# Gated cross-attention layer: the row table made by ScalarE before the branch, counting of places for slots two to four by six comparisons, and a changed order at the start

## The chip, the cores and the metric

The kernel runs on one NeuronCore of a Trainium2 chip. The metric is the time of one execution on the device, in microseconds (us). Before the change it is 656.4 us, the median of three runs (655.87 to 658.57). Engines are named as the profile names them: PE is TensorE (its weight loads are listed as PEld), DVE is VectorE, ACT is ScalarE, POOL is GpSimd, and SP only issues DMAs.

## The reference

There are 16 batches. Each has 224 rows of x (512 features) and a context of 750 rows (384 features), of which a mask keeps some. The layer is cross-attention with a gate, then a feed-forward network with weights rounded to -1, 0, 1 and rows rounded to 8 bits, with a second gate:

```python
sim  = einsum('bihd,bjhd->bhij', q, k) * 64**-0.5        # q from layernorm(x), k and v from the context
sim  = where(mask[:, None, None, :], sim, -finfo.max)
out  = einsum('bhij,bjhd->bihd', softmax(sim), v) @ W_o + b_o
x    = x + tanh(g_xattn) * out
# bitlinear: act_quant(rmsnorm(x)) against weight_quant(w), then + b
x    = x + tanh(g_ffn) * bitlinear(gelu(bitlinear(layernorm(x), w1, b1)), w2, b2)
```

`weight_quant` scales a whole weight matrix by the mean of its absolute values, so all of w1 must have been loaded and summed before any of it can be rounded; the same holds for w2.

## The kernel before, in words

**Sorting the batches.** `order_batches` loads the mask, counts the kept context rows of each batch and sorts the batches by that count. Position s in the sorted list is called slot s. `CAPS` gives each slot a number of context rows that it may use at most. A number `n_odd` tells whether all batches fit; every engine loads it (line 436) and branches on it (line 437). With these inputs the compact path is taken.

Only kept context rows are fetched. For slot s a table `upto` holds running counts of kept rows, in six parts of 125 rows (`NJ` = 6). The step `ind` compares the places 0 to 191 with that table, the step `pi` lets PE sum the comparisons over partitions, and the step `keys` makes row numbers of the sums. POOL then gathers these rows by an indirect DMA (`fetch_keys`, line 1055). Rows of x are gathered in sorted order in the same way (`fetch_x`, line 975), from a table `token`, which is made from `slots` by `spread` and one DVE operation (lines 265 to 270 and 343).

**Slot 0** is handled before the branch by `first_slot` (lines 1030 to 1055): six comparisons into six tiles; then for each half (128 and 64 places) six matmuls into one column of the PSUM tile `pi_0`, a DVE operation that makes the half's keys, and the gather. For the **other slots** `ind` is one comparison (line 1080) and five that also add what is there already (line 1082), into one tile with a single buffer; `pi` is then one matmul for each half (line 1091), and `keys` is line 1105.

**After the branch** the order of all work is written out by hand, as a string of step names (`ORDER`). Each step issues its instructions, its DMAs too, on the engines it uses, and every engine works through its own instructions in that order. A tile can be reused only when its readers are done. Steps that matter here:

- `hold.0` lets ACT read the first gathered context row, so that the loads after it on SP (`load.wv`, then `w.0.0` to `w.0.7`, the eight 512 KB pieces of w1) do not start before that gather has landed.
- `tokens` makes the token table on DVE. `stats.0.0`, `stats.0.1`, `rstd`, `norm.0.0` and `norm.0.1` normalise the first two tiles of x (lines 1258 to 1272); the power of -1/2 in it is POOL's (line 1267).
- `x.2.0` and other `x` steps are gathers of x, `ctx.1.0` and other `ctx` steps are gathers of context. All of them are issued by POOL.
- `warm` is eight matmuls whose result nobody uses (line 2137). `xnp` and `ctxp` are PE transposes of x and context (lines 1323 and 1160); `qp`, `kp` and `vp`/`vr` are the projections (lines 1345, 1180, 1207, 1224); `sim` are the scores (line 1378).
- `ws.0.*` sum the pieces of w1, some on ACT (line 2009) and some on DVE (line 2006). `wt.0` adds the sums, `wtp.0` is PE's matmul over partitions (line 2024) and `sw.0` makes the scale. After it come the rounding on DVE (`wi`, `wq`, lines 2047 and 2053), DMA transposes (`wd`, line 2061) and copies into `w1T` (`wT`). The same is done for w2 afterwards, in the same eight buffers; its `wtp.1` stands about 34 us later.

From there on the attention of a slot, the output projection and the feed-forward network of pairs of row tiles run interleaved to the end.

Of the kernel before, what the change touches and what calls it, by code (L numbers as in the profile page):

```python
# [10 lines left out]
BF16 = mybir.dt.bfloat16  # L11
AF = mybir.ActivationFunctionType
ALU = mybir.AluOpType
# [13 lines left out]
CAPS = (188, 188, 184, 180, 176, 168, 156, 148, 128, 124, 116, 104, 92, 80, 64, 64)  # L27

ORDER = """
hold.0 load.wv tokens stats.0.0 stats.0.1 rstd.0.0 rstd.0.1 x.2.0 norm.0.0 norm.0.1 ind.1 warm xnp.0 xnp.1 xnT.0.0:s  # L30
xnT.1.0:s xnT.1.1:s gap mask.0 ctxp.0.2 ctxp.0.0 qp.0.0 pi.1 ctxT.0.0:s ctxT.0.2:s keys.1 w.0.0 w.0.1 w.0.2 w.0.3
w.0.5 w.0.7 w.0.4 w.0.6 x.2.1 ctx.1.0 kp.0.0 ind.2 pi.2 x.1.0 x.1.1 ind.3 ws.0.1:s keys.2 stats.2.1 ctx.2.0 tanh
ws.0.0:v x.3.0 kp.0.2 kT.0.0:s stats.2.0 qT.0.0:s kT.0.0.c:s stats.1.1 rstd.2 ws.0.3:s sim.0.1 ws.0.2:v sim.0.0
ctx.1.1 kT.0.2:s ws.0.5:s vp.0 max.0.0.0 max.0.0.1 max.0.0.3 kT.0.2.c:s stats.1.0 exp.0.0.0 exp.0.0.1 max.0.1.0 rstd.1
exp.0.0.3 vr.0 max.0.0.2 v.0:s max.0.1.3 exp.0.0.2 norm.1.0 ws.0.4:v qp.0.2 v_rest.0:s norm.1.1 ws.0.7:s rec.0.0
# [172 lines left out]
def order_batches(ctx, tc, sh, mask, x, loads, fetch, first_slot):  # L208

    nc = tc.nc  # L210
    P = 128
    B, J = mask.shape
    S = x.shape[1]
    NJ = 6
    TJ = J // NJ
# [45 lines left out]
    for p, q, t in bounds:  # L261
        numbers(at[p:q, :, t : t + 1], [[7 * P - 4 * S, 4]], p + t * P - (t + 1) // 2 * S, 1)

    def spread(dst, src, on):

        by4 = src.rearrange("p (g s) -> p g s", s=4)
        on.tensor_copy(dst.rearrange("p g (s two) -> p g s two", two=2), by4.unsqueeze(3).to_broadcast([P, 4, 4, 2]))

        for p, q, t in bounds:
            on.tensor_copy(dst[p:q, :, t : t + 1], by4[p:q, :, (t + 1) // 2 : (t + 1) // 2 + 1])  # L270

    m = sel.tile([B, J], F16, name="m")
    kept = sel.tile([B, 1], F32, name="kept_of")
# [57 lines left out]
    spare = ps.tile([P, P], F32, name="spare")  # L331
    for k in range(3):
        nc.tensor.matmul(spare, lhsT=sh.ones, rhs=sh.ones, start=True, stop=True)
    first_slot(sel, ps)
    numbers(sh.place_f[:, :192], [[1, 192]], 0, 0)
    numbers(sh.place_f[:, 192:], [[1, P]], 0, 0)
    nc.gpsimd.memset(sh.mhalf, -0.5)
    where = const.tile([P, 4, 8], F32, name="where")
    sh.token = const.tile([P, 4, 8], mybir.dt.int32, name="token")

    def tokens():
        spread(where, sh.slots[:, 1, :], nc.vector)
        nc.vector.scalar_tensor_tensor(
            sh.token.rearrange("p g t -> p (g t)"),
            where.rearrange("p g t -> p (g t)"),
            float(S),
            at.rearrange("p g t -> p (g t)"),
            ALU.mult,
            ALU.add,
        )  # L350

    sh.tokens = tokens


class Shared:
# [3 lines left out]
@with_exitstack  # L359
def flamingo_gated_kernel(  # L360
    ctx: ExitStack,
    tc: tile.TileContext,
    x: bass.AP,
    context: bass.AP,
    mask: bass.AP,
    g_xattn: bass.AP,
    g_ffn: bass.AP,
    w_q: bass.AP,
    w_k: bass.AP,
    w_v: bass.AP,  # L370
    w_o: bass.AP,
    b_o: bass.AP,
    w1: bass.AP,
    b1: bass.AP,
    w2: bass.AP,
    b2: bass.AP,
    out: bass.AP,
):
    nc = tc.nc
    P = 128  # L380
    D = x.shape[2]
    C = context.shape[2]
    FF = w1.shape[0]
    ND, NC, NF = D // P, C // P, FF // P

    sh = Shared()
    sh.FF, sh.D = FF, D
    sh.const = const = ctx.enter_context(tc.tile_pool(name="const", bufs=1))
    sh.w1_dram, sh.w2_dram = w1, w2


    sh.ident = const.tile([P, P], F32, name="ident")
    sh.ident16 = const.tile([P, P], BF16, name="ident16")
    sh.ones = const.tile([P, P], F32, name="ones")
    sh.mhalf = const.tile([P, 2], F32, name="mhalf")
    sh.wk = const.tile([P, NC, D], F32, name="wk_sb")
    sh.wv = const.tile([P, NC, D], F32, name="wv_sb")
    sh.wq = const.tile([P, ND, D], F32, name="wq_sb")
    sh.wo = const.tile([P, ND, D], F32, name="wo_sb")
    sh.w1T = const.tile([P, ND, FF], F8, name="w1T")  # L400
    sh.w2T = const.tile([P, NF, D], F8, name="w2T")
    sh.bo = const.tile([P, D], F32, name="bo_bc")
    sh.b1 = const.tile([P, FF], F32, name="b1_bc")
    sh.b2 = const.tile([P, D], F32, name="b2_bc")
    sh.tgates = const.tile([P, 2], F32, name="tgates")
    sh.gates = gates = const.tile([P, 2], F32, name="gates")

    def loads():
        nc.sync.dma_start(sh.wq, w_q.rearrange("(c p) i -> p c i", p=P))
        nc.sync.dma_start(sh.wk, w_k.rearrange("(c p) i -> p c i", p=P))  # L410
        nc.sync.dma_start(gates[:, 0:1], g_xattn.partition_broadcast(P))
        nc.sync.dma_start(gates[:, 1:2], g_ffn.partition_broadcast(P))

    def late_loads(crossed):
        nc.sync.dma_start(sh.bo, b_o.partition_broadcast(P))
        nc.sync.dma_start(sh.b2, b2.partition_broadcast(P))
        by = w_o.rearrange("(c p) i -> p c i", p=P)
        if crossed:

            h = P // 2  # L420
            nc.sync.dma_start(sh.wo[:, 0:2, :], by[:, 0:2, :])
            nc.sync.dma_start(sh.wo[:h, 2:4, :], by[h:, 2:4, :])
            nc.sync.dma_start(sh.wo[h:, 2:4, :], by[:h, 2:4, :])
        else:
            nc.sync.dma_start(sh.wo, by)
        nc.sync.dma_start(sh.b1, b1.partition_broadcast(P))

    def load_wv():
        nc.sync.dma_start(sh.wv, w_v.rearrange("(c p) i -> p c i", p=P))

    stages = []
    compact = compact_path(ctx, tc, sh, x, context, out, dict(w_o=w_o, b_o=b_o, b1=b1, b2=b2, wv=load_wv), stages)
    with tc.manual_schedule(), ExitStack() as stage:
        fetch, first_slot = next(compact)
        order_batches(stage, tc, sh, mask, x, loads, fetch, first_slot)
    n_odd = nc.values_load(sh.n_odd[0:1, 0:1], min_val=0, max_val=2 * x.shape[0])
    with tc.If(n_odd == 0) as few:
        with ExitStack() as stage:
            stages.append(stage)
            next(compact, None)  # L440
    with few.Else():
        with ExitStack() as stage:
            late_loads(False)
            load_wv()
            sh.tokens()
            dense_path(stage, tc, sh, x, context, mask, out)


# [475 lines left out]
def compact_path(ctx, tc, sh, x, context, out, late_rows, stages):  # L924
# [67 lines left out]
    def rows_of(s, t):  # L992
        return min(width(s) - t * P, P)
# [38 lines left out]
    def first_slot(sel, ps):  # L1032
        ind = sel.tile([TJ, NJ, 192], BF16, name="ind_0")
        for n in range(NJ):
            nc.vector.tensor_scalar(ind[:, n, :], sh.place[:TJ], sh.upto[:, n, 0:1], None, ALU.is_ge)
        pi = ps.tile([P, 2], F32, name="pi_0")
        live[0]["ctx"] = kept = early[:, 2 * D : 2 * D + 2 * C].rearrange("p (t c) -> p t c", t=2)
        keys = sh.const.tile([P, 2], I32, name="keys_0")
        for t in range(2):
            rows = rows_of(0, t)  # L1040
            for n in range(NJ):
                nc.tensor.matmul(
                    pi[:rows, t : t + 1],
                    lhsT=ind[:, n, t * P : t * P + rows],
                    rhs=sh.one[:, 0:1],
                    start=(n == 0),
                    stop=(n == NJ - 1),
                )
            nc.vector.tensor_scalar(
                keys[:rows, t : t + 1], pi[:rows, t : t + 1], float(J - 1), sh.first[:rows, 0:1], ALU.min, ALU.add  # L1050
            )
            fetch_keys(kept[:rows, t, :], keys[:rows, t : t + 1])

    def fetch_keys(dst, at):
# [6 lines left out]
            oob_is_err=False,  # L1061
        )

    def select(s):
        if s == B - 1:
            return
# [7 lines left out]
        if s > 0:  # L1074
            @step("ind", s)
            def run():
                st["ind"] = ind = pa.tile([TJ, 192], BF16, tag="ind", name=f"ind_{s}", bufs=1)
                for b, at in parts:
                    place = sh.place[:TJ, : at.stop - at.start]
                    nc.vector.tensor_scalar(ind[:, at], place, sh.upto[:, 0, b : b + 1], None, ALU.is_ge)  # L1080
                    for n in range(1, NJ):
                        nc.vector.scalar_tensor_tensor(
                            ind[:, at], place, sh.upto[:, n, b : b + 1], ind[:, at], ALU.is_ge, ALU.add
                        )

            @step("pi", s)
            def run():
                st["pi"] = gen([P, 2], F32, f"pi_{s}")
                for t in range(nt):
                    rows = rows_of(s, t)  # L1090
                    nc.tensor.matmul(
                        st["pi"][:rows, t : t + 1],
                        lhsT=st["ind"][:, t * P : t * P + rows],
                        rhs=sh.one[:, 0:1],
                        start=True,
                        stop=True,
                    )

            @step("keys", s)
            def run():  # L1100
# [1032 lines left out]
    @step("warm")  # L2133
    def run():
        spare = gen([P, P], F32, "warm")
        for k in range(8):
            nc.tensor.matmul(spare, lhsT=sh.ones, rhs=sh.ones, start=True, stop=True)

    @step("tokens")
    def run():  # L2140
        sh.tokens()

    @step("load", "wv")
    def run():
# [71 lines left out]
```

## Time and profile before

| what | value |
|---|---|
| median of three runs | 656.4 us (655.87 to 658.57) |
| the profiled execution, its own time | 658.56 us |
| its span in the profile | 656.8 us |
| PE busy | 633.6 us, 96% |
| DVE busy | 494.2 us, 75% |
| ACT busy | 434.7 us, 66% |
| POOL busy | 380.8 us, 58% |
| PE busy between 100 and 650 us | 547.0 of 550 us |
| PE busy between 0 and 40 us | 30.1 of 40 us |

The span is what the profile covers; the execution's own time is 1.8 us longer. An idle stretch is put down to what ended it. PE's idle time lies almost wholly in the first 72 us: between 100 and 650 us it idles for 3 us. In a line of the timeline the first number is the start of a group of like instructions in us, the second its length; in square brackets stands how long the engine sat idle before it and what it waited for.

### The profile page before, as it was taken

How to read it: one execution, taken by the hardware profiler on the slowest of the kernel's cores; microseconds unless marked ns; L12 is line 12 of the kernel's file. 1: busy time of each engine (PE TensorE's matmuls, PEld its weight loads, DVE VectorE, ACT ScalarE, POOL GpSimd, SP SyncE). 2: the span in 40 equal slices, each digit the busy share in tenths (PEclk: the TensorE clock that was granted, in tenths of full speed). 3: DMA queues.
4: the chain of work that ended last, by engine and by line, in shares of the span. 5: the costliest groups of instructions: out<-in, count | busy, mean ns of one | idle time of the engine just before them, and what ended most of it. 6: DMA issues, size and time to landing. Idle time of an engine off the chain costs nothing.

```text
span 656.8 us, 11053 instructions
## 1 busy us (share of the span) xinstructions
PE 633.6 (96%) x3706; PEld 411.8 (63%) x3706; DVE 494.2 (75%) x1325; ACT 434.7 (66%) x985; POOL 380.8 (58%) x531
## 2 busy tenths in 40 slices
PE   6989899999999999999999999999999999999995
PEld 5767757767566585675756668656666755654442
DVE  6798788776874787777878577886595865858994
ACT  2489786767676673596757467875496554859694
POOL 6444558664866447663757763753776364564741
PEclk9999999999999999999999999999999999999999
DMA  6959682116233053312235521513243041433222
GB/s 204 371 81 304 196 199 69 45 49 110 66 87 86 32 80 91 84 34 61 65 77 80 96 75 34 92 46 58 64 117 73 17 97 50 95 65 81 48 33 86
DMA packets 97346, 60.73 MB, mean 92 GB/s; under 512 B 85461, under 2 KB 85609, under 8 KB 97152
## 3 DMA queue, kind: packets, MB, share of 16 engines
q1 hardware_dynamic: 89232, 35.41, 25.8%
q0 software_dynamic: 8048, 24.53, 12.4%
q8 instruction: 31, 0.51, 0.3%
q14 instruction: 35, 0.29, 0.1%
HBM read 31.87 MB, written 7.34 MB: 60 GB/s over the span
## 4 chain that ended last, share of the span: by engine, by line
PE 84%; DVE 6%; DMA 5%; ACT 2%; issue 1%; POOL 1%; DVEq 0%; POOLq 0%
PE hp L1671 14%; PE fp L1908 14%; PE qp L1345 14%; PE op L1547 13%; PE kp L1180 5%; PE vp L1207 5%; PE sim L1378 5%; PE ptp L1448 3%; PE av L1488 3%; DMA raw<-w 2%; PE xnp L1323 2%; DMA raw<-in_L_ffn_w_dram 2%; PE vr L1224 1%; DMA x<-in_x_dram,token 1%; PE ctxp L1160 1%
## 5 line engine op out<-in xcount | busy, mean ns | idle before, releaser
L1426 POOL TENSOR_TENSOR p<-p,rec 112x752 f32<-112x752 f32 (+13 forms) x64 | 73.2, 1149 | 134.4 <-DVE rec L1421 101.6
L1409 ACT ACTIVATE p<-p,nm 112x188 f32<-112x188 f32 (+13 forms) x256 | 102.0, 401 | 26.8 <-DVE nm L1395 25.8
L1345 PE MATMUL qp<-xnT,wq_sb 128*128 128x224 f32 x512 | 103.2, 355 | 0.0
L1671 PE MATMUL hp<-w1T,xqT 128*128 128x512 fp8e4 x448 | 102.1, 379 | 1.1 <-DVE h L1682 0.7
L1908 PE MATMUL fp<-w2T,hqT 128*128 128x512 fp8e4 x448 | 100.9, 379 | 0.7 <-ACT hqT L1713 0.7
L1547 PE MATMUL op<-wo_sb,xoT 128*128 128x512 f32 x224 | 101.0, 596 | 0.0
L1345 PEld LDWEIGHTS qp<-xnT,wq_sb 128*128 128x128 f32 x512 | 95.4, 190 | 4.9 <-issue 2.9
L1682 DVE SCALAR_TENSOR_TENSOR h<-hp,c,b_bc 128x1024 f32<-128x1024 f32 x52 | 66.6, 1282 | 31.3 <-PE hp L1671 26.5
L1671 PEld LDWEIGHTS <-xqT 128*128 128x128 bf16 x448 | 43.5, 98 | 51.3 <-issue 3.4
L1908 PEld LDWEIGHTS <-hqT 128*128 128x128 bf16 x448 | 43.1, 98 | 49.9 <-issue 1.1
L1547 PEld LDWEIGHTS op<-wo_sb,xoT 128*128 128x128 f32 x224 | 41.0, 190 | 44.7 <-issue 43.5
L1395 DVE CUSTOM_DVE_ANT_0 p<-sim,mask 112x64 f32<-112x64 f32 (+12 forms) x224 | 54.9, 281 | 18.7 <-PE sim L1378 12.0
L1731 DVE TENSOR_REDUCE a<-h 128x1 f32<-128x2048 f32 x26 | 59.2, 2277 | 1.1 <-ACT h L1726 1.1
L1726 ACT ACTIVATE h<-h 128x2048 f32<-128x2048 f32 x26 | 49.7, 1913 | 11.6 <-DVE h L1682 11.4
L1180 PE MATMUL kp<-ctxT,wk_sb 128*128 128x188 f32 (+12 forms) x360 | 52.4, 295 | 0.9 <-ACT pT L1025 0.9
L1180 PEld LDWEIGHTS kp<-ctxT,wk_sb 128*128 128x128 f32 x360 | 49.2, 191 | 5.9 <-issue 3.3
L1025 ACT COPY pT<-ptp 128x448 f32<-128x448 f32 (+6 forms) x54 | 28.1, 528 | 32.1 <-PE ptp L1448 30.1
L1409 ACT ACTIVATION_READ_ACCUMULATOR p<-p,nm 112x1 f32 x256 | 48.7, 190 | 0.0
L1757 ACT ACTIVATE h<-h 128x2048 f32<-128x2048 f32 x25 | 47.8, 1911 | 1.0 <-DVE hq L1737 1.0
L1378 PE MATMUL sim<-kT,qT 64*112 64x188 f32 (+13 forms) x512 | 42.5, 296 | 0.9 <-ACT xoT L1025 0.6
L1646 POOL TENSOR_TENSOR y<-y,b_bc 128x512 f32<-128x512 f32 x28 | 36.1, 1295 | 12.1 <-DVE xoT L1023 9.4
L1207 PE MATMUL vp<-wv_sb,ctxT 128*128 128x512 f32 (+5 forms) x90 | 41.6, 598 | 0.0
(211 smaller groups left out, 1161.4 us busy)
## 6 DMA issues: line engine op xcount, KB each, us to landing
raw<-in_L_ffn_w_dram SPq DMA_DIRECT2D x16, 512.0 KB, 5.5
wq_sb<-in_L_xattn_W_q_dram SPq DMA_DIRECT2D x1, 1024.0 KB
b_bc<-in_L_ffn_b_dram SPq DMA_DIRECT2D x1, 1024.0 KB
wk_sb<-in_L_xattn_W_k_dram SPq DMA_DIRECT2D x1, 768.0 KB
wv_sb<-in_L_xattn_W_v_dram SPq DMA_DIRECT2D x1, 768.0 KB
wo_sb<-in_L_xattn_W_o_dram SPq DMA_DIRECT2D x1, 512.0 KB, 11.6
wo_sb<-in_L_xattn_W_o_dram SPq DMA_DIRECT2D x2, 256.0 KB
out_dram<-y SPq DMA_DIRECT2D x2, 256.0 KB
```

The source lines that it names most:

```text
L1180: nc.tensor.matmul(pk[:, p - p0, :], lhsT=sh.wk[:, c, p * P : (p + 1) * P], rhs=st["ctxT"][:, c, :n], start=(c == 0), stop=(c == NC - 1),)
L1207: nc.tensor.matmul(pv[:w], lhsT=st["ctxT"][:, c, :w], rhs=sh.wv[:, c, :], start=(c == 0), stop=(c == NC - 1))
L1345: nc.tensor.matmul(pq[:, i, :], lhsT=sh.wq[:, d, (p + i) * P : (p + i + 1) * P], rhs=st["xnT"][:, d, :], start=(d == 0), stop=(d == ND - 1),)
L1378: nc.tensor.matmul(sim[:, j, i, :cap], lhsT=st["qT"][j * DH : (j + 1) * DH, p, q * TQ : (q + 1) * TQ], rhs=keys["kT"][j * DH : (j + 1) * D ...
L1395: nc.vector.tensor_tensor_reduce(out=probs[:, h, :cap], in0=box["sim"][:, j, i, :cap], in1=keys["mask"][:, first + j * begin : first + j * ...
L1409: nc.scalar.activation(box["p"][:, h, :cap], box["p"][:, h, :cap], AF.Exp, bias=box["nm", h], scale=-1.0, accum_out=total[:TQ, h : h + 1],)
L1426: nc.gpsimd.tensor_tensor(probs[:, :, first : first + cap], probs[:, :, :cap], box["rec"][:TQ].unsqueeze(2).to_broadcast([TQ, 4, cap]), AL ...
L1547: nc.tensor.matmul(po, lhsT=xoT[:, d, at : at + P], rhs=sh.wo[:, d, :], start=(d == 0), stop=(d == ND - 1))
L1671: nc.tensor.matmul(ph[:, n, :], lhsT=f["xqT"][:, k * ND + d, :], rhs=w1T[:, d, at : at + NB], start=(d == 0), stop=(d == ND - 1),)
L1682: nc.vector.scalar_tensor_tensor(h[:, cols], f["hp", k, g].rearrange("t i n -> t (i n)"), f["c1", k], sh.b1[:, cols], ALU.mult, ALU.add,)
L1731: nc.vector.tensor_reduce(amax[:, part], f["h", k], AX.X, ALU.max, apply_absolute_value=True)
L1908: nc.tensor.matmul(po, lhsT=f["hqT", k][:, n, :], rhs=w2T[:, n, :], start=(n == 0), stop=(n == NF - 1))
```

## The change

- **Token table.** `spread` runs on ACT (five copies) and stands before `first_slot` and so before the branch. The operation that makes `token` follows `first_slot` on DVE, before the branch. The step `tokens` is gone.
- **Slot 0.** All twelve matmuls of `pi_0` are issued first, and the two `keys` operations with their gathers after them. On POOL the two `place_f` tables and `mhalf` now come ahead of these gathers.
- **Slots 1 to 3** (`APART` = 3). `ind` is six separate comparisons into a tile with six parts (one buffer, tag `ind6`), and `pi` is six matmuls for each half, twelve in all.
- **Order.** `x.2.0` stands ahead of `stats.0.0` (it was behind `rstd.0.1`). `pi.1` stands ahead of `qp.0.0` (it was behind); `keys.1` ahead of the copies `ctxT.0.*`; `ind.2` ahead of the loads `w.0.*` (it was behind `kp.0.0`). On DVE and ACT the order among the remaining instructions is as it was.
- **Warm.** Six matmuls in the place of eight.

```diff
 ORDER = """
-hold.0 load.wv tokens stats.0.0 stats.0.1 rstd.0.0 rstd.0.1 x.2.0 norm.0.0 norm.0.1 ind.1 warm xnp.0 xnp.1 xnT.0.0:s
-xnT.1.0:s xnT.1.1:s gap mask.0 ctxp.0.2 ctxp.0.0 qp.0.0 pi.1 ctxT.0.0:s ctxT.0.2:s keys.1 w.0.0 w.0.1 w.0.2 w.0.3
-w.0.5 w.0.7 w.0.4 w.0.6 x.2.1 ctx.1.0 kp.0.0 ind.2 pi.2 x.1.0 x.1.1 ind.3 ws.0.1:s keys.2 stats.2.1 ctx.2.0 tanh
+hold.0 load.wv x.2.0 stats.0.0 stats.0.1 rstd.0.0 rstd.0.1 norm.0.0 norm.0.1 ind.1 warm xnp.0 xnp.1 xnT.0.0:s
+xnT.1.0:s xnT.1.1:s gap mask.0 ctxp.0.2 ctxp.0.0 pi.1 qp.0.0 keys.1 ctxT.0.0:s ctxT.0.2:s ind.2 w.0.0 w.0.1 w.0.2
+w.0.3 w.0.5 w.0.7 w.0.4 w.0.6 x.2.1 ctx.1.0 kp.0.0 pi.2 x.1.0 x.1.1 ind.3 ws.0.1:s keys.2 stats.2.1 ctx.2.0 tanh
...
-    def spread(dst, src, on):
+    def spread(dst, src):
         by4 = src.rearrange("p (g s) -> p g s", s=4)
-        on.tensor_copy(dst.rearrange("p g (s two) -> p g s two", two=2), by4.unsqueeze(3).to_broadcast([P, 4, 4, 2]))
+        nc.scalar.copy(dst.rearrange("p g (s two) -> p g s two", two=2), by4.unsqueeze(3).to_broadcast([P, 4, 4, 2]))
         for p, q, t in bounds:
-            on.tensor_copy(dst[p:q, :, t : t + 1], by4[p:q, :, (t + 1) // 2 : (t + 1) // 2 + 1])
+            nc.scalar.copy(dst[p:q, :, t : t + 1], by4[p:q, :, (t + 1) // 2 : (t + 1) // 2 + 1])
...
-    first_slot(sel, ps)
     numbers(sh.place_f[:, :192], [[1, 192]], 0, 0)
     numbers(sh.place_f[:, 192:], [[1, P]], 0, 0)
     nc.gpsimd.memset(sh.mhalf, -0.5)
...
-    def tokens():
-        spread(where, sh.slots[:, 1, :], nc.vector)
-        nc.vector.scalar_tensor_tensor(
...
-    sh.tokens = tokens
+    spread(where, sh.slots[:, 1, :])
+    first_slot(sel, ps)
+    nc.vector.scalar_tensor_tensor(
+        sh.token.rearrange("p g t -> p (g t)"),
+        where.rearrange("p g t -> p (g t)"),
+        float(S),
+        at.rearrange("p g t -> p (g t)"),
+        ALU.mult,
+        ALU.add,
+    )
...
                     start=(n == 0),
                     stop=(n == NJ - 1),
                 )
+        for t in range(2):
+            rows = rows_of(0, t)
             nc.vector.tensor_scalar(
                 keys[:rows, t : t + 1], pi[:rows, t : t + 1], float(J - 1), sh.first[:rows, 0:1], ALU.min, ALU.add
             )
...
+    APART = 3
...
             @step("ind", s)
             def run():
+                if s <= APART:
+                    st["ind"] = ind = pa.tile([TJ, NJ, 192], BF16, tag="ind6", name=f"ind_{s}", bufs=1)
+                    for n in range(NJ):
+                        nc.vector.tensor_scalar(ind[:, n, :], sh.place[:TJ], sh.upto[:, n, s : s + 1], None, ALU.is_ge)
+                    return
...
                 for t in range(nt):
                     rows = rows_of(s, t)
-                    nc.tensor.matmul(
-                        st["pi"][:rows, t : t + 1],
-                        lhsT=st["ind"][:, t * P : t * P + rows],
-                        rhs=sh.one[:, 0:1],
-                        start=True,
-                        stop=True,
-                    )
+                    for n in range(NJ if s <= APART else 1):
+                        ind = st["ind"][:, n, :] if s <= APART else st["ind"]
+                        nc.tensor.matmul(
+                            st["pi"][:rows, t : t + 1],
+                            lhsT=ind[:, t * P : t * P + rows],
+                            rhs=sh.one[:, 0:1],
+                            start=(n == 0),
+                            stop=(s > APART or n == NJ - 1),
+                        )
...
-        for k in range(8):
+        for k in range(6):
             nc.tensor.matmul(spare, lhsT=sh.ones, rhs=sh.ones, start=True, stop=True)
```

More of the change, by code (lines that the diff above doesn't have):

```diff
@@ L339, in order_batches @@
     sh.token = const.tile([P, 4, 8], mybir.dt.int32, name="token")
-    def tokens():
-        spread(where, sh.slots[:, 1, :], nc.vector)
-        nc.vector.scalar_tensor_tensor(
[L344 to L349, printed above, removed]
-        )
-    sh.tokens = tokens
+    spread(where, sh.slots[:, 1, :])
[8 more added lines that the diff above has]
+    )
 class Shared:
@@ L444, in flamingo_gated_kernel @@
             load_wv()
-            sh.tokens()
             dense_path(stage, tc, sh, x, context, mask, out)
@@ L1090, in run @@
                     rows = rows_of(s, t)
-                    nc.tensor.matmul(
-                        st["pi"][:rows, t : t + 1],
-                        lhsT=st["ind"][:, t * P : t * P + rows],
-                        rhs=sh.one[:, 0:1],
-                        start=True,
-                        stop=True,
-                    )
+                    for n in range(NJ if s <= APART else 1):
[7 more added lines that the diff above has]
+                        )
             @step("keys", s)
@@ L2135, in run @@
         spare = gen([P, P], F32, "warm")
-        for k in range(8):
+        for k in range(6):
             nc.tensor.matmul(spare, lhsT=sh.ones, rhs=sh.ones, start=True, stop=True)
-    @step("tokens")
-    def run():
-        sh.tokens()
     @step("load", "wv")
```

## The prediction

> **What bounds the kernel.** First the page.
>
> ```profile
> PE 633.6 (96%) x3706; PEld 411.8 (63%) x3706; DVE 494.2 (75%) x1325; ACT 434.7 (66%) x985; POOL 380.8 (58%) x531
> PE 84%; DVE 6%; DMA 5%; ACT 2%; issue 1%; POOL 1%; DVEq 0%; POOLq 0%
> ```
>
> PE is the bound, and the chain that ended last lies on it for 84%. Free time on another engine is therefore worth nothing by itself; the change can move the end only through PE's idle time, 23 us in all, or by giving PE more work. Second, who PE waited for, in its first 100 us (columns: total us, times, longest).
>
> ```profile
> PE wtotp L2024 <- DVE wtot L2019: 4.5, 2, 2.7
> PE pi L1091 <- DVE ind L1082: 0.8, 1, 0.8
> ```
>
> The change touches the second wait. The first is where the start of the kernel meets the rest: PE arrives at the sum of the w1 weights 2.73 us early. Third, the chain in order of time (start, length).
>
> ```profile
> 35.96 1.14 DVE wsums L2006
> 37.10 0.03 issue
> 37.15 0.05 issue
> 37.20 0.17 DVE wtot L2019
> 37.37 0.14 issue
> 37.50 0.37 PE wtotp L2024 x2
> ```
>
> DVE sets 37.50. From there to the w2 sum at 71.75 rounding, transposing and loading follow one another on DVE, DMA and ACT, PE has 0.93 and 1.76 us idle in it, and later almost none. So I ask one thing: when does DVE reach `wtot`? A shift there goes through to the end. Fourth, the timeline of the start.
>
> ```profile
> 8.89 0.22 DVE L1049 TENSOR_SCALAR keys<-pi,first 128x1 int32<-128x1 f32 x1 [0.35 <-PE pi L1042]
> 9.16 0.43 PE L1042 MATMUL pi<-one,ind 125*64 125x1 bf16 x6 [0.38 <-DVE keys L1049]
> 9.38 1.00 POOL L1055 DMA_INDIRECT xoT<-in_ctx_dram,keys  x1 [0.96 <-DVE keys L1049]
> 12.79 0.59 POOL L1267 TENSOR_TENSOR rs_x<-rs_x,mhalf 128x1 f32<-128x1 f32 x1 [0.54 <-DVE rs_x L1262]
> 14.15 2.13 PE L1323 MATMUL xnp<-ident,xoT 128*128 128x128 f32 x8 [0.26 <-DVE xoT L1272]
> 14.68 1.08 POOL L975 DMA_INDIRECT x<-in_x_dram,token  x1 [0.18 <-issue]
> 23.80 0.27 DVE L1080 TENSOR_SCALAR ind<-place,upto 125x192 bf16<-125x192 bf16 x1 [0.39 <-PE pi L1091]
> 30.05 0.69 DVE L1292 BATCH_NORM_STATS2 bs_x<-x 128x6 f32<-128x512 f32 x1 [0.70 <-DMA x<-in_x_dram,token]
> ```
>
> Read here that POOL is busy with gathers just before it computes the norm's power, and that DVE's last wait before `wtot` is 0.70 us for a gather of x; from 30.05 to 37.2 it never waits.
>
> **The parts, on the profiled execution** (658.56 us of its own, span 656.8; 2.2 above the median of 656.4).
>
> *Slot 0's keys.* The first `keys` now waits for twelve matmuls; the second six cost 0.43 us, so it starts 0.40 later, near 9.30. The second is ready 0.1 earlier, but its gather stands behind the first on POOL. Both gathers move 0.40: 9.78 and 11.09, the second ending at 12.05. `place_f` and `mhalf` (0.55) fit into POOL's 0.96 wait. `hold.0` releases SP's wv and w1 loads 0.40 later; against that, the 256 KB of `x.2.0` go ahead of them at a time when DMA is idle (share 0.26 between 12 and 14 us), 0.7 us at the 385 GB/s of 16 to 30 us. Cost taken: 0, within -0.3 and +0.4.
>
> *Token table.* Five ACT copies of about 0.2 (the rows beside them: 0.19, 0.22) lie in ACT's 4.95 us wait before 12.49: free; uncovered they would cost 1. DVE loses 1.2 us of work after the branch, and both `stats` come 1.1 earlier. Nothing comes of it, for POOL is next.
>
> *`x.2.0` ahead of the power.* After the gathers POOL takes about 0.52 for the branch (DVE: 9.84 to 10.36) and starts `x.2.0` at 12.6; its 1.08 end near 13.7. Only then come the powers, 13.75 to 14.34 and to 15.15, though their input is ready at 11.5 and 12.6. Behind them wait `norm.0.0`, `norm.0.1`, then `xnp` on PE: 15.11 in the place of 14.15 (+0.96), its second half at 15.84 (+0.65). `x.2.1` is issued at 15.2 (was 16.06).
>
> *Warm.* Four records of 0.234 less: 0.94 of useless PE work gone, but PE then stands idle from 12.6 to 15.1. This bears on the clock. The granted clock reads 1.00 all along, yet the durations change:
>
> ```profile
> L2137 PE MATMUL warm<-ones x16: 421/421/553, 10.1 to 13.5; 128*128 128x128 f32 x16
> L1323 PE MATMUL xnp<-ident,xoT x8: 397/421/477, 14.2 to 15.9; 128*128 128x128 f32 x8
> L1160 PE MATMUL ctxp<-ident,xoT x6: 223/273/328, 16.1 to 17.0; 128*128 128x128 f32 x3, 64*128 64x64 f32 x3
> ```
>
> Transposes take 421 ns up to 15.9 and 273 from 16.1 on: PE's speed rises at 16.1, 5.9 us after `warm` began. If PE needs as long a run again, beginning at 15.1, its speed is low until 21.0. Bounds: 16.1 as now, and 26 (a run that begins after `pi.1`, whose one-column matmuls may not count, and takes 6 us or more). I take 21.0, as a repetition of the only rise there is.
>
> [...]
>
> *Slots 1 to 3.* On DVE six comparisons cost 1.19 (slot 0's row) in the place of 0.26 + 2.23: 1.3 less for each slot. On PE twelve matmuls cost twice 0.43 in the place of 0.14 to 0.29: 0.7 more for each. `ind.1` is ready at 17, ahead of need; its gain is hidden. `ind.3` shares the one buffer and waits for all of `pi.2`, and `keys.2`, `stats.2.1`, `ws.0.0`, `stats.2.0`, `stats.1.1` queue behind it on DVE. `pi.3` (56.1) pays 0.7 on PE ahead of idle stretches of 0.93 and 1.76: free, otherwise +0.7.
>
> *The path, clock rising at 21.0.* `xnp` ends at 16.9; `ctxp` at low speed 1.5 (at full speed 0.95), 18.4; `pi.1` 19.3; `qp.0.0` (3.2 at full speed; at low speed 16 records of 0.234 x 224/128 = 0.41 at most, 0.37 by columns alone, 6.0) does 1.7/6.0 of its work by 21.0, ends at 23.3; `kp.0.0` 2.1, 25.4; `pi.2` 0.9, 26.3; `ind.3` 1.2, 27.5; `keys.2` 27.6 (was 26.25): +1.35. From there DVE ran 3.1 us to the end of its queue at 29.35 and waited 0.70: `stats.1.1` comes at 30.7, +0.65. Its gather, `x.1.1`, cannot hold it: `keys.1` at 19.4 lets POOL issue it at 22.5 (was 23.72). `wtot` moves by 0.65, `wtotp` to 38.15; PE (`kp.0.2` 28.4, `sim` 29.9, `vp` 32.6, `vr` 34.1, `qp.0.2` 37.3) is still there first. **Sum: +0.65 us**, 659.2 on the profiled execution and 657.1 against the median.
>
> **Rivals.**
>
> *Earlier (-0.85).* PE has its full speed from 16.1. `pi.2` ends at 24.7, `keys.2` starts at 26.1, the gather of `x.1.1` goes out 2 us earlier, so DVE's 0.70 wait goes as well: `stats.1.1` at 29.2, 655.5. For it: the idle ends 0.1 us before the old moment of rise. Against: the rise came only after `warm` and `xnp` had run nearly without a gap.
>
> *Much earlier (-4.5).* Both waits for `wtot` vanish: 652. Against: DVE has no idle time left from 30.05 to 37.2, and w2's sum ended on a load. Only far quicker w1 loads would do it.
>
> *Slower: the rise comes late.* This is the rival on the other side. With the rise at 22.9 the same walk gives `keys.2` 28.5 and +1.55; at 26 all of `qp.0.0` runs at low speed (25.3), `kp.0.0` ends at 27.7, `pi.2` 28.6, `keys.2` 29.95, `stats.1.1` 33.05: +3.0, 659.4. About 0.47 us for each us; it passes 0.5% (3.3 us) when the rise comes after 26.6. For it: a gap of 2.5 us, and 24 tiny matmuls among the first work. Against: `qp.0.0` alone keeps PE dense for up to 6 us.
>
> *The change does not free what it says.* DVE's 1.2 + 3 x 1.3 us are real but end in waits for POOL and PE. That is part of the forecast; if nothing else moved, 656.4.
>
> **Chances and range.** A measurement tells about 0.5%, 3.3 us, from no change. Forecast (rise between 18 and 23, or nothing moves) 0.45; earlier 0.17; much earlier 0.08; late 0.30, of which I give 0.10 to a rise before 26.6 and 0.20 to a later one, or to a second fall that the one trace cannot exclude. So faster 0.08, same 0.45 + 0.17 + 0.10 = 0.72, slower 0.20. Range: -0.85 and +3.0 around 656.4 are 655.5 and 659.4; with 0.9 and 1.0 for the spread of the runs (655.87 to 658.57), 654.6 to 660.4. That leaves out the much earlier case and half of the latest.
>
> **What would show it.** `keys` of slot 0 at 9.3; `x.2.0` on POOL before the first L1267, which ends after 14.2; PE idle of about 2.5 us before `xnp`, starting at 15.1; transposes in `ctxp` at 421 ns and not 273, the first records of `qp` above 352; no wait of `pi.2` for `ind`; `keys.2` between 27 and 28.5; `wtotp` near 38.1. Wrong would make it: PE at full speed when `xnp` starts, a POOL branch shorter than 0.5, or PE arriving at `wtotp` after DVE.

## The result, and the profile after

The changed kernel takes 658.2 us (median; 656.78 to 661.06) where the kernel before took 656.39 on the same chip: a ratio of 1.0024, 95% interval 1.0015 to 1.0034. That is some 1.6 us slower: within the 0.5% that the prediction called "same", but told apart from no change by these runs. The two profiled executions do not show this difference: the one of before, at 658.56 us, was at the top of its runs' range (655.70 to 658.57), and the one of after has 658.17 us, span 656.4. A second trace of the kernel before follows with the experiments.

The page of after, the lines of busy time and of the chain that ended last:

```profile
PE 635.4 (97%) x3732; PEld 413.8 (63%) x3732; DVE 490.1 (75%) x1320; ACT 435.5 (66%) x990; POOL 379.8 (58%) x531
PE 85%; DVE 6%; DMA 3%; ACT 2%; issue 2%; POOL 0%; DVEq 0%; POOLq 0%; ACTq 0%
```

DVE lost 4.1 us of work and nothing came of it; PE is the bound as before, with 1.8 us more of busy time for 26 more matmuls. Its waits in the first 100 us (total, times, longest):

```profile
PE xnp L1330 <- DVE xoT L1279: 2.0, 1, 2.0
PE wtotp L2031 <- DVE wtot L2026: 1.6, 2, 1.1
PE kp L1187 <- ACT pT L1021: 1.4, 1, 1.4
```

The wait of `pi` for `ind` (0.8) is gone. In its place is a wait of 2.0 before the first transposes, and the waits for the two weight sums have shrunk from 4.5 to 1.6: PE comes to them later. The chain at the w1 sum (start, length):

```profile
36.19 1.14 DVE wsums L2013
...
37.44 0.17 DVE wtot L2026
...
37.74 0.35 PE wtotp L2031 x2
```

37.74, where the prediction had 38.15 and the trace of before 37.50. Now the start, in the timeline:

```profile
9.36 0.34 DVE L1047 TENSOR_SCALAR keys<-pi,first 128x1 int32<-128x1 f32 x2 [0.76 <-PE pi L1038]
9.84 2.90 PE L2144 MATMUL warm<-ones 128*128 128x128 f32 x12 [0.59 <-DVE token L342]
12.43 1.01 POOL L971 DMA_INDIRECT x<-in_x_dram,token  x1 [0.30 <-DVE rs_x L1269]
13.46 1.21 POOL L1274 TENSOR_TENSOR rs_x<-rs_x,mhalf 128x1 f32<-128x1 f32 x2
14.70 1.97 PE L1330 MATMUL xnp<-ident,xoT 128*128 128x128 f32 x8 [1.95 <-DVE xoT L1279]
18.13 0.73 PE L1098 MATMUL pi<-one,ind 125*128 125x1 bf16 x12
18.79 5.09 PE L1352 MATMUL qp<-xnT,wq_sb 128*128 128x224 f32 x16
26.23 1.16 DVE L1080 TENSOR_SCALAR ind<-place,upto 125x192 bf16<-125x192 bf16 x6 [5.84 <-PE pi L1098]
27.32 0.33 DVE L1112 TENSOR_SCALAR keys<-pi,first 128x1 int32<-128x1 f32 x2
```

Read from the top: the gather `x.2.0` holds POOL until 13.44, both powers stand behind it, PE stands idle for 1.95 us, and the first `qp` takes 5.09 us instead of 3.29. The durations by tile (least, median and longest ns, first and last start) say why:

```profile
L1330 PE MATMUL xnp<-ident,xoT x8: 420/421/477, 14.7 to 16.2; 128*128 128x128 f32 x8
L1167 PE MATMUL ctxp<-ident,xoT x6: 311/394/474, 16.5 to 17.9; 128*128 128x128 f32 x3, 64*128 64x64 f32 x3
L1352 PE MATMUL qp<-xnT,wq_sb x16: 352/581/738, 18.8 to 23.5; 128*128 128x224 f32 x16
```

All transposes and most of `qp.0.0` ran at PE's low speed: up to 22.3 the matmuls of `qp.0.0` start 0.373 us apart, from 22.6 on 0.190. The clock record in the packed trace agrees: its first entry, at full clock, begins at 22.46, and at 16.13 in the trace of before. Moments of the rise below are read from these first entries.

### The profile page after: what moved, and what is told of

It is laid out like the page before. It is cut to its first block, busy times and chain, and to the rows that moved or that the text cites. A ratio compares the mean times of both kernels' runs of the same rounds, so it can differ in the third digit from the quotient of the medians.

```text
span 656.4 us, 11106 instructions
## 1 busy us (share of the span) xinstructions
PE 635.4 (97%) x3732; PEld 413.8 (63%) x3732; DVE 490.1 (75%) x1320; ACT 435.5 (66%) x990; POOL 379.8 (58%) x531
## 4 chain that ended last, share of the span: by engine, by line
PE 85%; DVE 6%; DMA 3%; ACT 2%; issue 2%; POOL 0%; DVEq 0%; POOLq 0%; ACTq 0%
PE hp L1678 14%; PE qp L1352 14%; PE fp L1915 14%; PE op L1554 13%; PE kp L1187 6%; PE vp L1214 5%; PE sim L1385 5%; PE ptp L1455 3%; PE av L1495 3%; PE xnp L1330 2%; DMA raw<-in_L_ffn_w_dram 2%; DMA raw<-w 1%; PE vr L1231 1%; PE ctxp L1167 1%; PE ptr L1469 1%
## 5 line engine op out<-in xcount | busy, mean ns | idle before, releaser
L1416 ACT ACTIVATE p<-p,nm 112x188 f32<-112x188 f32 (+13 forms) x256 | 102.0, 401 | 24.9 <-DVE nm L1402 23.8
L1352 PE MATMUL qp<-xnT,wq_sb 128*128 128x224 f32 x512 | 105.0, 359 | 0.0
L1352 PEld LDWEIGHTS qp<-xnT,wq_sb 128*128 128x128 f32 x512 | 96.8, 193 | 5.2 <-issue 2.5
L971 POOL DMA_INDIRECT y<-in_x_dram,token x28 | 32.9, 1174 | 15.4 <-DMA out_dram<-y,token 7.7
```

Of the source, the lines that this page charges most:

```text
L1352: nc.tensor.matmul(pq[:, i, :], lhsT=sh.wq[:, d, (p + i) * P : (p + i + 1) * P], rhs=st["xnT"][:, d, :], start=(d == 0), stop=(d == ND - 1),)
L1416: nc.scalar.activation(box["p"][:, h, :cap], box["p"][:, h, :cap], AF.Exp, bias=box["nm", h], scale=-1.0, accum_out=total[:TQ, h : h + 1],)
```

## The experiments

**Theory:** the loss comes from PE's idle stretch before `xnp`, made by two matmuls fewer in `warm` and by `x.2.0` ahead of the powers; the low speed lasts longer and moves the w1 sum. **Rivals:** the six comparisons with their twelve matmuls cost it; the order on POOL costs it by itself; there is no loss but the spread of the runs. Every kernel was timed in five rounds, in three groups, against runs of the kernel before on the same chip (medians 656.6, 657.16 and 657.42). So ratios are compared, not medians.

### Filling the idle stretch, undoing parts of the change

The kernel before again, unedited:

> The kernel before, unchanged, for a second trace: the profiled execution shown before the change took 658.56 us, 2.2 above the median of its runs. All theories: ratio 1.000. Clock theory (the moment at which PE's matmuls become shorter differs from run to run, and the start of the kernel follows it): a trace of an execution near 656.4 us shows transposes of 273 ns before 16.1 us, and the w1 sum on PE 1 to 2 us before 37.5. If instead the executions differ somewhere after 72 us, the clock theory is wrong about the spread.

The changed kernel with the gather behind the work for the powers:

```diff
-hold.0 load.wv x.2.0 stats.0.0 stats.0.1 rstd.0.0 rstd.0.1 norm.0.0 norm.0.1 ind.1 warm xnp.0 xnp.1 xnT.0.0:s
+hold.0 load.wv stats.0.0 stats.0.1 rstd.0.0 rstd.0.1 x.2.0 norm.0.0 norm.0.1 ind.1 warm xnp.0 xnp.1 xnT.0.0:s
```

> The changed kernel with the gather x.2.0 behind the two powers again. POOL theory (the loss comes from POOL issuing x.2.0 ahead of the powers, which delays the first transposes): the transposes start near 13.8 in the place of 14.7, and the loss of 1.8 us is gone to at least 1 us, 656.4 to 657.2. Clock theory: PE's gap before them shrinks from 1.95 to about 1.0 us, which helps by 0.5 to 1. Matmul theory (30 more small matmuls on PE cost what they last): no change, 658.2.

The changed kernel with ten idle matmuls, all else as it is:

```diff
-        for k in range(6):
+        for k in range(10):
             nc.tensor.matmul(spare, lhsT=sh.ones, rhs=sh.ones, start=True, stop=True)
```

> The changed kernel with ten idle matmuls in the place of six, 20 records of 0.234 us from 9.84 to about 14.5, so that PE does not stand idle before the first transposes. Clock theory: PE's matmuls become short before 17 us in nearly every run, qp.0.0 takes 3.3 us and not 5.1, and the time falls by 1 to 2 us, to 656.2 to 657.2. POOL and matmul theories: no change, 658.2.

The changed kernel with the comparisons of slots 1 to 3 as they were:

```diff
-    APART = 3
+    APART = 0
```

> The changed kernel with the comparisons of slots 1 to 3 added up on DVE again (two matmuls each in the place of twelve), all else as changed. Matmul theory: PE is relieved of about 0.4 to 0.6 us three times, 656.4 to 657. Clock theory: a quarter to half of this, 657.7 to 658.2, through an earlier start of qp.0.0. POOL theory: no change, 658.2.

| kernel | median us | ratio to before | interval |
|---|---|---|---|
| before again | 657.08 | 1.0005 | 0.9995 to 1.0016 |
| after, `x.2.0` behind | 657.52 | 1.0017 | 1.0004 to 1.0029 |
| after, ten idle matmuls | 656.95 | 0.9997 | 0.9985 to 1.001 |
| after, comparisons undone | 658.51 | 1.0036 | 1.0021 to 1.005 |

The repeat of before gives a second trace of the same code, of an execution of 655.98 us. As the first trace came from an execution longer than the median of before, this one comes from a shorter one: 0.4 us below the 656.39 of the first comparison, 1.1 below the repeat's own median. Its timeline on PE at the start:

```profile
14.12 0.66 PE L1323 MATMUL xnp<-ident,xoT 128*128 128x128 f32 x4 [0.27 <-DVE xoT L1272]
16.69 3.29 PE L1345 MATMUL qp<-xnT,wq_sb 128*128 128x224 f32 x16
36.92 0.35 PE L2024 MATMUL wtotp<-wtot,ones 128*128 128x1 f32 x2 [2.62 <-DVE wtot L2019]
```

Same code, but PE is at its higher speed by 14.12 already (four transposes in 0.66 us; the rise is at 13.78), and the w1 sum comes at 36.92 instead of 37.50. Against this trace the changed kernel, whose traced execution lies at its median, is 0.82 us late at the w1 sum, 1.42 at the w2 sum (71.97 against 70.55) and 2.2 in the span.

Ten idle matmuls take the loss away: the interval does not meet that of the changed kernel. Here the comparisons are still apart and `x.2.0` is still ahead of the powers. Its timeline:

```profile
13.37 1.20 POOL L1274 TENSOR_TENSOR rs_x<-rs_x,mhalf 128x1 f32<-128x1 f32 x2
14.59 1.27 PE L1330 MATMUL xnp<-ident,xoT 128*128 128x128 f32 x8 [0.51 <-DVE xoT L1279]
17.25 3.29 PE L1352 MATMUL qp<-xnT,wq_sb 128*128 128x224 f32 x16
36.56 0.35 PE L2031 MATMUL wtotp<-wtot,ones 128*128 128x1 f32 x2 [1.76 <-DVE wtot L2026]
```

The powers are as late as in the changed kernel and `xnp` starts only 0.11 earlier, but the gap is 0.51, the speed is up, and `qp.0.0` takes 3.29. So the late powers, and all else that this kernel keeps of the change, cost nothing that shows as long as there are enough idle matmuls. With `x.2.0` behind, the opposite: `xnp` starts at 13.38 after a gap of 0.66, and PE is still slow:

```profile
13.38 1.97 PE L1330 MATMUL xnp<-ident,xoT 128*128 128x128 f32 x8 [0.66 <-DVE xoT L1279]
17.46 5.75 PE L1352 MATMUL qp<-xnT,wq_sb 128*128 128x224 f32 x16
```

So a short gap alone does not help. With ten idle matmuls the rise, at 13.69, comes while they still run (until 14.09), ahead of any gap; with six it comes at 22.49 here. Whether six fail because they are few or because of the gap behind them was not separated: no run has six without a gap. The 1.0017 overlaps the changed kernel's 1.0024; what the gather's place is worth alone stays open. Undoing the comparisons does not help (1.0036, overlapping as well), so the loss does not come from them.

### The suspected edit alone

The kernel before with fewer idle matmuls and nothing else, four of them (shown) and six, the change's own number:

```diff
-        for k in range(8):
+        for k in range(4):
```

> The kernel before with four idle matmuls in the place of eight and nothing else of the change: PE stands idle for about 2 us before the first transposes (from about 12.0 to 14.15), as it does in the changed kernel. Clock theory: the gap alone brings most of the loss, PE's transposes stay at 421 ns through ctxp, qp.0.0 takes 4 to 5 us, and the time is 657.4 to 658.4 (+0.8 to +1.8). If the loss came from the order on POOL, the later gathers or the extra matmuls, it stays at 656.4 to 656.8.

> The kernel before with six idle matmuls in the place of eight, which is the change's own edit of them, alone: idle matmuls end near 13.0, a gap of 1.2 us before the transposes at 14.15. Clock theory: between eight (1.000) and four (1.0024); 1.0005 to 1.002, with low speed through qp.0.0 in part of the runs. If the gap matters only from 2 us on, 1.000, and then it takes the later power on POOL as well to lose.

And the other part alone: the six comparisons for slots 1 to 3 in the kernel before, as in the change's diff (`APART = 3`, `ind`, `pi`).

> The kernel before with the six separate comparisons for slots 1 to 3 alone. Undone in the changed kernel, they made it 0.3 us slower (658.51 against 658.20, on different chips). Clock theory with this part as a small gain: the wait of pi.2 for ind.2 (0.77 us) goes, keys.2 comes up to 0.7 us earlier, and the ratio is 0.999 to 1.000. Matmul theory (30 more matmuls cost 0.45 to 0.6 us each): 1.001 to 1.003.

| kernel | median us | ratio to before | interval |
|---|---|---|---|
| before, four idle matmuls | 659.16 | 1.0024 | 1.0006 to 1.0041 |
| before, six idle matmuls | 659.32 | 1.0029 | 1.0014 to 1.0044 |
| before, comparisons apart | 657.72 | 1.0006 | 0.9996 to 1.0017 |

Two useless matmuls fewer, 0.85 us of work (2.90 for 3.75), make the kernel before 0.29% slower: as large a loss as the whole change's. Six cost no less than four, though they were expected to lie between four and eight; the intervals overlap. The timeline with six:

```profile
14.09 2.16 PE L1323 MATMUL xnp<-ident,xoT 128*128 128x128 f32 x8 [1.11 <-DVE xoT L1272]
17.71 4.82 PE L1345 MATMUL qp<-xnT,wq_sb 128*128 128x224 f32 x16
22.36 0.29 PE L1091 MATMUL pi<-one,ind 125*128 125x1 bf16 x2
39.35 0.35 PE L2024 MATMUL wtotp<-wtot,ones 128*128 128x1 f32 x2 [2.51 <-DVE wtot L2019]
```

`xnp` starts when it did before (14.09 against 14.12), the speed rises at 20.83, and `pi.1`, which stands behind `qp.0.0` in the old order, slips to 22.36 (19.82 in the repeat). Behind `pi.1` wait `keys.1`, then POOL's gathers, then DVE. Its chain shows where that lands:

```profile
31.90 0.70 DVE bs_x L1292
...
39.04 0.17 DVE wtot L2019
```

`stats.1.1` comes at 31.90, after 0.48 of waiting for its gather, and the w1 sum at 39.35, 2.4 later than in the repeat. In the changed kernel, at as low a speed, it is 37.74: there `pi.1` stands ahead of `qp.0.0`, and `stats.1.1` starts at 30.32 with no wait. That the new order limits the loss is read from single traces; the ratios overlap.

### Filling, and going past the kernel before

If the gap is the cost, the change with the gap closed and `x.2.0` behind the powers might win. Five kernels tried this, or a second gap at the w1 sum: the edit of `x.2.0` above with eight idle matmuls; the same with `ws.0.1` and `tanh` moved behind the first three copies on ACT, which PE was found waiting for; and idle matmuls ahead of the w1 sum, since PE waits there, in each of these and in the kernel before.

> The changed kernel with x.2.0 behind the powers and eight idle matmuls, so that the transposes come near 13.5 and no gap lies before them. Clock theory with the order on POOL as the second part: both losses are gone, qp.0.0 takes 3.3 us in most runs, 655.8 to 656.6, not slower than the kernel before. Rival, the twelve matmuls and the later gather cost something of their own: 656.8 to 657.5, no better than ten idle matmuls alone.

> The kernel before with six idle matmuls (about 2.3 us) put on PE just ahead of the w1 sum, into the wait of 2.6 to 2.7 us. Clock theory, second place (that wait lets PE's clock fall in part of the runs: granted clock 0.72 between 36 and 42 us in two of the traces so far): the granted clock there is 1.00, the transposes after it last 273 ns, and the time falls by 0.3 to 1.0 us and spreads less, 655.4 to 656.1. Rival (PE has slack enough behind that point, the fall is absorbed by the wait for the w2 sum): no change, 656.4.

> The kernel of x2_warm8 with five idle matmuls ahead of the w1 sum as well. Clock theory: both falls are gone, this is the fastest of all, 655.0 to 656.0. Rival of slack: as x2_warm8.

The idle matmuls ahead of the w1 sum, six in the kernel before (shown), five and eight in the other two:

```diff
-            box["pt"] = pt = gen([P, 1], F32, f"wtotp_{wi}")
+            tile = gen([P, P], F32, f"wtotp_{wi}")
+            for k in range(6 if wi == 0 else 0):
+                nc.tensor.matmul(tile, lhsT=sh.ones, rhs=sh.ones, start=True, stop=True)
+            box["pt"] = pt = tile[:, 0:1]
```

The order on ACT:

> x2_warm8 with the first weight sum on ACT (and tanh) behind the three copies of kT and qT of slot 0. In x2_warm8 PE stood 1.94 us before sim, for ACT was still waiting for the first piece of w1 to land (23.6), and PE's matmuls after it were long again (vp 4.02 us in the place of 2.84). With the wait gone PE is at the w1 sum near 33 and DVE decides it: 36.0 to 36.5 in the place of 36.62. Clock theory: no fall at sim, but a wait of about 3 us and a fall at the w1 sum; 656.0 to 656.8, ratio 0.998 to 1.000. If the clock plays no part here: 0.998.

```diff
-w.0.3 w.0.5 w.0.7 w.0.4 w.0.6 x.2.1 ctx.1.0 kp.0.0 pi.2 x.1.0 x.1.1 ind.3 ws.0.1:s keys.2 stats.2.1 ctx.2.0 tanh
-ws.0.0:v x.3.0 kp.0.2 kT.0.0:s stats.2.0 qT.0.0:s kT.0.0.c:s stats.1.1 rstd.2 ws.0.3:s sim.0.1 ws.0.2:v sim.0.0
+w.0.3 w.0.5 w.0.7 w.0.4 w.0.6 x.2.1 ctx.1.0 kp.0.0 pi.2 x.1.0 x.1.1 ind.3 keys.2 stats.2.1 ctx.2.0
+ws.0.0:v x.3.0 kp.0.2 kT.0.0:s stats.2.0 qT.0.0:s kT.0.0.c:s ws.0.1:s tanh stats.1.1 rstd.2 ws.0.3:s sim.0.1 ws.0.2:v sim.0.0
```

> The same with eight idle matmuls (16 records of 0.125 us, 2.0 us) ahead of the w1 sum, where PE now has about 3 us of true idle time, so that they delay nothing. Clock theory: the granted clock between 36 and 42 us stays 1.00, the fastest of all, ratio 0.997 to 0.999. If filling a wait costs in itself, as five idle matmuls did behind a late PE (1.0022): not faster than x2_warm8_ws.

| kernel | median us | ratio to before | interval |
|---|---|---|---|
| after, `x.2.0` behind, eight idle | 656.64 | 0.999 | 0.9977 to 1.0002 |
| before, six ahead of the w1 sum | 658.19 | 1.0014 | 0.9999 to 1.0028 |
| after, `x.2.0` behind, eight, five ahead of the sum | 659.02 | 1.0022 | 1.0007 to 1.0036 |
| after, `x.2.0` behind, eight, ACT order | 657.75 | 1.0008 | 0.9999 to 1.0018 |
| the same, eight ahead of the sum | 657.34 | 1.0003 | 0.9991 to 1.0014 |

None is clearly faster than before; the first is the best and its interval reaches past 1. The other four were expected to beat the kernel before and did not. Its timeline shows where the earlier start went:

```profile
13.41 1.27 PE L1330 MATMUL xnp<-ident,xoT 128*128 128x128 f32 x8
25.72 2.38 PE L1385 MATMUL sim<-kT,qT 64*112 64x188 f32 x16 [1.94 <-ACT qT L1021]
28.04 4.02 PE L1214 MATMUL vp<-wv_sb,ctxT 128*128 128x512 f32 x6
33.52 1.22 DVE L2013 TENSOR_REDUCE wsums<-raw 128x1 f32<-128x1024 f32 x1 [2.54 <-DMA raw<-in_L_ffn_w_dram]
36.62 0.35 PE L2031 MATMUL wtotp<-wtot,ones 128*128 128x1 f32 x2
```

PE is done with `kp.0.2` near 23.8, waits 1.94 for an ACT copy, and then `sim` takes 2.38 and `vp` 4.02, against 1.53 and 2.84 in the repeat of before: the clock record has half clock from 27.03 to 30.44. ACT was held up in `ws.0.1`, the sum of a w1 piece that landed only at 23.63. With ACT's order changed that wait is gone and PE reaches the w1 sum early, and waits there:

```profile
33.14 1.22 DVE L2013 TENSOR_REDUCE wsums<-raw 128x1 f32<-128x1024 f32 x1 [1.64 <-DMA raw<-in_L_ffn_w_dram]
36.43 0.56 PE L2031 MATMUL wtotp<-wtot,ones 128*128 128x1 f32 x2 [3.01 <-DVE wtot L2026]
39.12 2.94 PE L1385 MATMUL sim<-kT,qT 64*112 64x188 f32 x16
```

3.01 us of waiting, and `sim` takes 2.94 after it. In the four of these five kernels where PE is not late, the sum comes at 36.43 to 36.87, and PE coming earlier gains nothing there. What sets it in the changed ones is a load: in all four of them, and with ten idle matmuls, DVE waits 1.64 to 2.93 us for a piece of w1 that lands between 33.1 and 33.8, and one more such sum and `wtot` follow on DVE. In the changed kernel itself DVE is busy from 26.23 to the sum and waits for no load. So a late start of PE delays the w1 sum, but a start earlier than in these kernels would end in the wait for the loads. Where PE is late the idle matmuls cost directly: with five, PE came to them at 36.87, and the sum followed at 37.99.

```profile
36.87 1.28 PE L2032 MATMUL wtotp<-ones 128*128 128x128 f32 x10
37.99 0.28 PE L2034 MATMUL wtotp<-wtot,ones 128*128 128x1 f32 x2
```

In the kernel before, six of them left 1.24 us to wait and no slow `sim` followed, but the time did not improve: in its trace the low speed came behind the wait of 1.76 at the w2 sum instead, where the next `qp` took 4.96 against 3.27 in the repeat. With eight, 2.10 us were left and `sim` took 2.93 again.

## Why the prediction was right or wrong

**Direction, range and mechanism held.** Predicted 657.1 (654.6 to 660.4) for 658.2; the forecast shift was +0.65, the measured one some +1.6 by the ratio, outside the forecast's own size though inside its range. PE idle before `xnp`, low speed through `ctxp` and into `qp.0.0`, then `pi.2`, `ind.3`, `keys.2`, `stats.1.1`: this walk is in the trace, step by step. That PE's late speed, and not the comparisons, costs the time was argued then and is shown now: the `warm` edit alone loses 0.29%, and four more idle matmuls in the changed kernel lose nothing. The number came near partly by luck: on the scale of the profiled execution the forecast, 659.2, was 1.0 too long (658.17), against the median, 657.1, it was 1.1 too short.

**Slot 0's keys, token table.** `keys` at 9.36 (said 9.30), the gathers at 9.85 and 11.17 (9.78, 11.09); ACT's copies (7.51 to 8.58) lay in its idle time, ahead of a wait of 4.53. SP's loads moved by 0.61 (13.41 against 12.80), not 0.40. The other places were right; what they cost was not measured apart.

**`x.2.0` ahead of the power.** "About 0.52 for the branch" was 0.30, and the two powers took 1.21 rather than 1.4, so `xnp` started at 14.70, not 15.11. The gap was 1.95, not 2.5. Order and consequence were right, the size too large by 0.4.

**Warm.** "I take 21.0": in the changed kernel the rise came at 22.46, and in the five traces with six or four idle matmuls between 20.83 and 22.49, so 21.0 was the early end. By the prediction's 0.47 us for each us that is 0.7 more; the earlier `xnp` and shorter `pi` records gave it back, and `keys.2` came 0.3 before its forecast.

**What was off most is the other end of the same term:** "PE's speed rises at 16.1" was taken as what the kernel before does. In the repeat it rises at 13.78, with the same code; in the two other kernels that leave PE's work up to there as it was (idle matmuls ahead of the w1 sum, comparisons apart) at 14.45 and 15.61, so 16.13 is the late end of four. The sum was made against an execution that had itself lost time against the repeat, 0.58 us at the w1 sum, 1.20 at the w2 sum and 2.6 at the end, and then carried over to the median as a shift. Against the repeat the changed kernel's loss at the w1 sum is not 0.24 but 0.82; as the repeat's execution was shorter than the median, 0.82 is probably too much. "A shift there goes through to the end" did not hold to the tenth either: to the w2 sum the difference grew to 1.42, and to 2.2 at the end. Over all 14 traces the stretch from the w1 to the w2 sum varies from 33.47 to 35.25 us and the rest from 583.4 to 585.7, which is as much as the effect. Where the part of the measured 1.6 beyond the w1 sum arises is not settled.

**Slots 1 to 3.** Six comparisons took 1.16 to 1.25 (said 1.19), `pi.2` 0.57 rather than 0.9, for at the higher speed its records are shorter than slot 0's (in the second half 170 ns, starting 0.031 us apart, against 192 ns and 0.053). The wait of DVE for `pi.2` grew to 5.84, as its single buffer made it. `keys.2` at 27.32 (27.6). In the kernel before the comparisons alone cost 1.0006, nothing that can be told from 1.

**From DVE to the w1 sum.** Said +0.65, seen +0.24 on the two profiled executions, +0.82 against the repeat. DVE's wait for the gather went, as written. PE "is still there first" held, with 0.54 to spare.

**Rivals.** "Earlier" and "much earlier" needed full speed from 16.1 or earlier loads; neither came. But the first is close to what ten idle matmuls made of it (0.9997). Its -0.85 is there at the w1 sum against the first trace of before (36.56 for 37.50), -0.36 against the repeat, and does not show in the time: DVE's wait for the gather went, and a wait of 1.72 for a piece of w1 took its place. What was held against "much earlier", "Only far quicker w1 loads would do it", is what these waits show. "Rise comes late" at 22.9 was given +1.55: by its moment, 22.46, and by the loss the result lies nearer to this rival than to the forecast. 0.45 for a rise between 18 and 23 covered it, the point value did not.

**The moment of the rise.** The clock record changes at whole multiples of 3.41 us after its first entry: 187 of them in the trace of before (638.29 us), 185 in that of after (631.47 us), and 4 in that of the changed kernel with `x.2.0` behind and eight idle matmuls (from the rise at 13.38 to the half clock at 27.03). The first entry begins at another moment in each trace, between 13.38 and 22.49. With `warm` 3.7 us or longer (eight idle matmuls or more) the speed rose between 13.38 and 16.13 in nine of nine traces; with 2.9 us or less (six or four) it did not rise before 20.83 in five of five, though the gap after it was only 0.66 us in one of them. From the end of the gap to the rise it took 6.3 us (comparisons undone), 6.7, 7.8, 7.9 and 9.1 (`x.2.0` behind), each longer than the 5.9 that the prediction took over from the trace of before. In the last three PE's records fill the whole 3.41 us before the rise, and the whole 3.41 us before those as well, which brought no rise; that earlier stretch holds transposes of `ctxp` each time, in two of the three also the twelve small matmuls of `pi`. What sets the moment is not shown.

## What to carry to other kernels

Idle matmuls ahead of the first real work are part of the schedule: two fewer of them, and PE's low speed lasted 4.7 us longer or more (20.83 against 13.78 to 16.13), which cost 0.29% of a kernel of 657 us. When a change touches them or delays the first real matmul, look at which speed PE does its first work, in the mean ns of one transpose and not in the clock row. And before a sum is made against one profiled execution, compare it with the median of the runs: here what it had lost was as large as the effect to be predicted.

## What was not expected of the hardware

**The low speed came back later on, behind seven of nine waits of PE of 1.7 to 3.6 us.** The repeat of before, on PE behind its wait of 2.62 us at the w1 sum:

```profile
37.76 1.11 PE L1323 MATMUL xnp<-ident,x 128*128 128x128 f32 x4
38.67 0.72 PE L1160 MATMUL ctxp<-ident,ctx 128*128 128x128 f32 x2
39.03 2.57 PE L1378 MATMUL sim<-kT,qT 64*112 64x188 f32 x16
```

The same lines in the first trace of before, behind 2.73 us of waiting:

```profile
38.33 0.66 PE L1323 MATMUL xnp<-ident,x 128*128 128x128 f32 x4
38.83 0.48 PE L1160 MATMUL ctxp<-ident,ctx 128*128 128x128 f32 x2
39.04 1.58 PE L1378 MATMUL sim<-kT,qT 64*112 64x188 f32 x16
```

The granted clock between 36 and 42 us is 0.72 in the one and 1.00 in the other, the third column from the right (stretch, busy time of each engine, clock, share and rate of DMA; the repeat first):

```profile
36.00:42.00 6.00, 5.08 (x33) 4.30 (x34) 5.46 (x16) 3.96 (x17) 2.16 (x3) 0.72 0.22 41
36.00:42.00 6.00, 4.50 (x41) 3.89 (x42) 5.46 (x13) 5.30 (x23) 2.77 (x3) 1.00 0.11 21
```

Over all traces: of nine waits between 1.7 and 3.6 us at the w1 sum, seven were followed by low speed within some 5 us and two were not; of the five traces with 1.3 us or less there, none. In the repeat the fall cost about 1.6 us (from the start of `ctxp` to that of the matmul behind `sim`, 4.40 against 2.83 in the first trace of before), and in five of the seven PE then came last to the w2 sum, where it otherwise had 0.4 to 1.8 us to spare. That these falls take back part of an earlier start is argued from single traces, beside the w1 loads, whose waits the traces show. The length of the wait does not decide alone: the stretch of 3.41 us before each of the seven falls held 0.80 to 1.96 us of PE work, but one of 1.57 (first trace of before) was followed by none. Six of the seven waits lasted 1.76 to 3.01 us, the seventh 3.56.

**The clock row does not show the low speed at the start.** It reads 1.00 between 10 and 14 us, in the traces of before and after as in four more, while the idle matmuls take 421 ns, as the slow transposes do, instead of 273; it shows only the later falls. The record behind it has no entry before the rise (16.13 in the trace of before, 22.46 in that of after), and the row counts such time as full clock.

**What stays open:** how much of the loss the place of `x.2.0` makes by itself, and whether the small matmuls of `pi` have a part in how late the rise comes. Neither was separated; `pi` is not needed for a late one, for in the kernel before with four idle matmuls none stands before the rise at 22.02.
